# Strassen's seven products for the keys and values of the second attention

## The chip, the cores and the metric

The kernel runs on one core of one Trainium2 chip. The metric is the device time of one execution in microseconds. The engines are TensorE (PE), VectorE (DVE), ScalarE (ACT) and GpSimd (POOL); SP issues most of the transfers. All arithmetic that this change touches is in 32-bit floats.

## The reference

The model is four layers, each a gated attention to a context and a gated feed-forward part, on x of 2 batches x 256 rows x 256 columns. The context has 2 batches x 512 rows x 256 columns. Two layers use the context in a form that matters here:

```python
    # layer 0: the context itself is key and value; layer 1: 16 heads of 128 columns
    def _L1_xattn_ref(inputs_q, inputs_kv, Wq, Wk, Wv, Wo):
        q = (inputs_q @ Wq).reshape(b, sq, H, HD) * (1.0 / np.sqrt(HD))
        k = (inputs_kv @ Wk).reshape(b, skv, H, HD)
        v = (inputs_kv @ Wv).reshape(b, skv, H, HD)
        scores = jnp.einsum('bqhd,bkhd->bhqk', q, k)
        attn = jax.nn.softmax(scores, axis=-1)
        ctx = jnp.einsum('bhqk,bkhd->bqhd', attn, v).reshape(b, sq, H * HD)
        return ctx @ Wo
    x = x + jnp.tanh(g_xattn[1]) * _L1_xattn_ref(_layernorm(x, axis=-1), ctx_2048, ...)
```

So the keys of one head are a product of the context (1024 rows in all, 256 columns) with 256 x 128 weights, and the values likewise. The 256 columns that are summed over are two halves of 128, the height of PE's array.

## The kernel before

The layers run one after the other. The text is Python that lists instructions; the framework then lays out an order for each engine's queue when the program is built, by when it reckons each instruction to be ready, with the place in the text deciding between instructions that are ready together. On the chip each queue runs in that fixed order, with waits on semaphores. A tile of a pool takes one of the pool's buffers at its first writing and gives it back after its last reading. Helpers named `inline` and `behind` pin some orders by hand, in the first attention above all; the second attention has no pins.

PSUM, which PE writes and from which VectorE and ScalarE read, is split during the second attention into `ps_mm` (4 buffers, line 530), `ps_tr` (2 buffers, line 531, for transposes) and `ps_acc` (2 buffers). In SBUF the pools `q2` (15 buffers of 2 KB per partition) and `q4` (11 of 4 KB) hold working tiles, and `slab` has 12 slots for weights.

The context lies in SBUF twice: `ctx_nat` (rows on partitions) is read by the scores of the first attention (line 438) and again at the end by the fourth attention (line 1248), which begins its reading at 527 us; `ctxT` (columns on partitions, two halves `k`) is read by all key and value products and by others.

The first attention (`l0_scores`, `l0_values`, `l0_join`, `l0_exchange`, `l0_finish`) ends on PE at about 56 us. The values of head group 0 (`l1_values_of(0)`, line 555) follow, then the first feed-forward part (`ternary_ffn`), whose signs GpSimd prepares in `ternary_below` (line 348) while the first attention runs.

The second attention has 16 heads in 4 groups `g` of 4 heads `hl`. A group's weights (queries, keys, values, output) are one load of 2 MB into two slots of the slab (`load_group`). For a head, in the order of the text (lines 673 to 691):

- queries: 2 products of 512 columns into one buffer of `ps_mm`, copied by ScalarE (line 681);
- for each batch `b`: `l1_scores`, 4 products of 256 columns into two buffers of `ps_mm`, exponentials by ScalarE (line 643), and their sums over rows by VectorE (lines 646, 647);
- `l1_attend`, one call late through `later`: 4 products of 256 columns with the values and one with ones, the reciprocal and a multiplication on VectorE (lines 655, 656), and two running sums on GpSimd (lines 657, 658), which later tell whether a general form of the kernel must run instead;
- `l1_keys_of(h + 2)`: the keys for the head after the next, for each batch 2 products of 512 columns, summed in PSUM and copied by ScalarE (line 551);
- in the group's second head, `l1_values_of(g + 1)`: 8 times 2 products of 512 columns, copied by ScalarE into slab slots 8 to 11 (line 542);
- after the group, `l1_out` (16 products of 256 columns, added to x on VectorE).

The first group's values and the first two heads' keys are made ahead of the loop. After the loop come the loads of the expert weights of layer 2 into slots 4 to 11 (line 695).

Of the kernel before, what the change touches and what calls it, by code (L numbers as in the profile page):

```python
# [17 lines left out]
F32 = mybir.dt.float32  # L18
# [7 lines left out]
P = 128  # L26
# [3 lines left out]
B = 2  # L30
M = 512
# [18 lines left out]
def flamingo(ctx: ExitStack, tc: tile.TileContext, a: dict, out: bass.AP):  # L50
    nc = tc.nc
# [6 lines left out]
    q4 = pool("q4", Q4)  # L58
    q2 = pool("q2", Q2)
# [32 lines left out]
    slab = const.tile([P, SLOTS, WCOLS], F32, name="slab")  # L92
# [17 lines left out]
    l1_w = [load_group(0), load_group(1)]  # L110
# [149 lines left out]
    def mm(shape=None):  # L260
        return ps_mm.tile(shape or [P, 512], F32, tag="mm", name="mm")
# [221 lines left out]
    for s in range(18):  # L483
# [3 lines left out]
        if 1 <= s <= 16:  # L487
            m, i, half = (s - 1) // 4, (s - 1) // 2 % 2, (s - 1) % 2
# [45 lines left out]
    HD = 128  # L534

    def l1_values_of(g):
        v = slab[:, 8 + 2 * (g % 2) : 10 + 2 * (g % 2), :].rearrange("p s (m c) -> p (s m) c", m=4)
        for mt in range(8):
            p = mm()
            chain(p, [(ctxT[:, mt // 4, k, mt % 4 * P : (mt % 4 + 1) * P], l1_w[g][2][:, k, :])  # L540
                      for k in range(2)])
            nc.scalar.copy(v[:, mt, :], p)  # L542
        return v

    def l1_keys_of(h):
        kT = q4.tile([P, B * M], F32, tag="q4", name="kT")
        for b in range(B):
            p = mm()
            chain(p, [(l1_w[h // 4][1][:, k, (h % 4) * HD : (h % 4 + 1) * HD], ctxT[:, b, k, :])
                      for k in range(2)])  # L550
            nc.scalar.copy(kT[:, b * M : (b + 1) * M], p)  # L551
        return kT


    v_next = l1_values_of(0)

    def transposed(pr, dst, view=None):
        tr = ps_tr.tile([P, 4, P], F32, tag="tr", name="tr")
        for c in range(4):
            inline(nc.tensor.transpose(tr[:, c, :], pr[:, c * P : (c + 1) * P] if view is None else view(pr, c), ident), pe_line)  # L560
        evict(dst, tr)
# [12 lines left out]
    def ternary_ffn():  # L574


        xs = [q4.tile([P, B, 2, 256], F32R, tag="q4", name="xs") for _ in range(2)]

        def split(n, tr):
            top = q1.tile([P, 2, P], F32, tag="q1", name="topx")  # L580
            nc.vector.tensor_scalar(top.bitcast(I32), tr.bitcast(I32), -4096, None, ALU.bitwise_and)
            nc.scalar.copy(tokens(xs[0], n), top)
            nc.vector.tensor_sub(tokens(xs[1], n), tr, top)

        norm_tiles(split, xn0)
# [12 lines left out]
        ps = {}  # L598
        for c, _, ts in by_batch(FCH):
            if c not in ps:  # L600
                ps[c] = mm(), mm()
            for w, p in zip((0, 2), ps[c]):
                chain(p[:, ts], [(signs[w + k][:, c * P : (c + 1) * P], batch(h, k, ts)) for k in range(2) for h in xs])
            if ts.stop == T:
                s = q2.tile([P, T], F32, tag="q2", name="silu")
                nc.scalar.activation(s, ps[c][0], AF.Silu, scale=scales[0])
                nc.vector.tensor_mul(s, s, ps[c][1])
                h = q4.tile([P, 2, T], F32R, tag="q4", name="hT")
                halves(h[:, 0, :], h[:, 1, :], s)
                later(lambda c=c, h=h: l0_down(c, h), 1)  # L610
        flush()
        for dh in range(2):
            p = outs[dh]
            o = q2.tile([P, T], F32, tag="q2", name="o0")
            nc.scalar.copy(o, p)
            tr = ps_tr.tile([P, NT, P], F32, tag="tr", name="tr")
            for n in range(NT):
                nc.tensor.transpose(tr[:, n, :], o[:, n * P : (n + 1) * P], ident)
            cols = x[:, :, dh * P : (dh + 1) * P]
            nc.vector.scalar_tensor_tensor(cols, tr, s2, cols, ALU.mult, ALU.add)  # L620


    ternary_ffn()
    l1_w += [load_group(2), load_group(3)]
    keys = deque(l1_keys_of(h) for h in range(2))
# [8 lines left out]
    def l1_scores(b, qT, kT):  # L634
        cols = slice(b * 256, (b + 1) * 256)
        es = []
        for half in range(2):
            s = mm([P, 2, D])
            for k in range(2):
                c = b * M + (2 * half + k) * P  # L640
                chain(s[:, k, :], [(kT[:, c : c + P], qT[:, cols])])
            e = q2.tile([P, 2, D], F32, tag="q2", name="e1")
            nc.scalar.activation(e, s, AF.Exp)  # L643
            es.append(e)
        t = q2.tile([P, 2, D], F32, tag="q2", name="t1")
        nc.vector.tensor_add(t, es[0], es[1])  # L646
        nc.vector.tensor_add(t[:, 0, :], t[:, 0, :], t[:, 1, :])  # L647
        return es, t

    def l1_attend(b, hl, v, es, t, oT):  # L650
        acc = ps_acc.tile([P, 2, D], F32, tag="acc", name="acc")
        chain(acc[:, 0, :], [(v[:, b * 4 + c, hl * HD : (hl + 1) * HD], es[c // 2][:, c % 2, :]) for c in range(4)])
        chain(acc[:, 1, :], [(ones, t[:, 0, :])])
        r = q1.tile([P, D], F32, tag="q1", name="r1")
        nc.vector.reciprocal(r, acc[:, 1, :])  # L655
        nc.vector.tensor_mul(oT[:, b * 256 : (b + 1) * 256], acc[:, 0, :], r)  # L656
        nc.gpsimd.tensor_add(all_t, all_t, t[:, 0, :])  # L657
        nc.gpsimd.tensor_add(all_r, all_r, r)  # L658

    def l1_out(g, oTs):  # L660
        wo = l1_w[g][3]
        for n in range(NT):
            acc = ps_acc.tile([P, D], F32, tag="acc", name="acc")
            chain(acc, [(oTs[hl][:, n * P : (n + 1) * P], wo[:, hl, :]) for hl in range(4)])
            add_to_x(n, acc, gx(1))

        if g == 0:
            ffn1.extend([load(0, "l1_gate"), load(1, "l1_up")])
        if g == 1:
            ffn1.extend([load(2, "l1_down"), load(3, "l2_attn")])  # L670

    ffn1 = []
    for g in range(4):
        v, oTs = v_next, []
        for hl in range(4):
            h = 4 * g + hl
            kT = keys.popleft()
            qT = q2.tile([P, T], F32, tag="q2", name="qT")
            p = mm()
            chain(p, [(l1_w[g][0][:, k, hl * HD : (hl + 1) * HD], batch(xT, k)) for k in range(2)])  # L680
            nc.scalar.activation(qT, p, AF.Copy, scale=HD ** -0.5)  # L681
            oT = q2.tile([P, T], F32, tag="q2", name="oT")
            oTs.append(oT)
            for b in range(B):
                es, t = l1_scores(b, qT, kT)
                later(lambda b=b, hl=hl, v=v, es=es, t=t, oT=oT: l1_attend(b, hl, v, es, t, oT), 1)
            if h < 14:
                keys.append(l1_keys_of(h + 2))
            if hl == 1 and g < 3:
                v_next = l1_values_of(g + 1)  # L690
        later(lambda g=g, oTs=oTs: l1_out(g, oTs), 2)
    flush()
    gu2 = slab[:, 4:12, :].rearrange("p e (w k i) -> p e w k i", w=2, k=2)
    for e in range(E):
        nc.sync.dma_start(slab[:, 4 + e, :], a["l2_gu_all"][e])
# [329 lines left out]
    t, u = rtile(), place  # L1025
# [1162 lines left out]
```

## Time and profile before

| | us |
|---|---|
| runs before: median of 3 (lowest to highest) | 612.91 (611.39 to 617.0) |
| the profiled execution's own time | 606.47 |
| its span on the core | 604.7 |
| PE busy | 577.8 |
| DVE busy | 279.0 |
| ACT busy | 194.9 |
| POOL busy | 139.9 |
| mean granted PE clock | 0.988 |

The profile is of one execution; its span is 1.8 us shorter than its time. "Busy" is the sum of the stretches in which an engine works; PE's weight loads run beside its products and are listed apart. In the lists, a product of the text with 32-bit floats stands as two matrix instructions. A group of instructions is named by line, engine, operation and tiles (out<-in), with count, busy time and the mean duration of one, and then the idle time ahead of it with what ended that. Line 265 is the helper `chain`, through which most products go.

### The profile page before, as it was taken

The page shows a single profiled execution, that of the slowest core. Times are in us where ns is not written, and L with a number is a line of the kernel's source. Part 1 is how long each engine was busy: PE and PEld are TensorE (multiplying, and loading weights), DVE is VectorE, ACT ScalarE, POOL GpSimd, SP SyncE. Part 2 cuts the span into 40 slices and gives each one's busy share as a digit, 9 for nine tenths or more (in the row PEclk, how much of TensorE's full clock was granted, in tenths as well). Part 3 has the DMA queues.
Part 4 walks back from the last instruction along what each step waited for, and adds up shares of the span by engine and source line. Part 5 has one row for each costly group of instructions (what it writes and reads, how often), then busy time and mean ns, then how long its engine had stood idle before and what let it go on. Part 6 is the DMA issues. An engine that isn't in the chain of part 4 may idle for free.

```text
span 604.7 us, 8168 instructions
## 1 busy us (share of the span) xinstructions
PE 577.8 (96%) x3142; PEld 380.1 (63%) x3142; DVE 279.0 (46%) x575; ACT 194.9 (32%) x369; POOL 139.9 (23%) x238
## 2 busy tenths in 40 slices
PE   8989998999999999999999998999999999899995
PEld 5544674656677466864678677648666445785454
DVE  6967343342534244350445557223566524554323
ACT  6855543433223233123331331220432311332220
POOL 3883152110211112020111213201011000243150
PEclk9979999999999999999999999999999999899998
DMA  8903300000201001010044014603120599804013
GB/s 302 379 2 124 156 0 1 0 1 1 69 2 69 1 0 69 10 60 1 1 140 139 0 70 148 218 15 131 63 65 6 221 419 412 212 22 135 17 41 119
DMA packets 14980, 58.06 MB, mean 96 GB/s; under 512 B 2621, under 2 KB 5892, under 8 KB 11302
## 3 DMA queue, kind: packets, MB, share of 16 engines
q1 hardware_dynamic: 12886, 52.65, 24.0%
q0 software_dynamic: 1472, 4.28, 2.2%
q8 instruction: 27, 0.44, 0.3%
q10 hardware_dynamic: 576, 0.53, 0.3%
q14 instruction: 19, 0.16, 0.1%
HBM read 52.65 MB, written 5.25 MB: 96 GB/s over the span
## 4 chain that ended last, share of the span: by engine, by line
PE 81%; DVE 7%; DMA 4%; POOL 4%; ACT 1%; issue 1%; SPq 0%; POOLq 0%; DVEq 0%
PE mm L265 46%; PE acc L265 18%; PE mm L1106 3%; PE mm L1434 2%; POOL tern L348 2%; DMA slab<-in_l_gu_all 2%; DMA slab<-in_l_gate 2%; PE s L438 2%; PE acc L450 1%; DVE x L268 1%; PE outT L595 1%; PE acc L1127 1%; PE acc L1456 1%; POOL rstd L220 1%; DVE r L655 1%
## 5 line engine op out<-in xcount | busy, mean ns | idle before, releaser
L646 DVE TENSOR_TENSOR t<-e,e 128x512 f32<-128x512 f32 x32 | 26.4, 826 | 138.0 <-ACT e L643 138.0
L265 PE MATMUL mm<-xT,slab 128*128 128x512 f32 (+1 forms) x236 | 85.2, 507 | 0.5 <-ACT xT L249 0.5
L265 PE MATMUL mm<-slab,ctxT 128*128 128x512 f32 x160 | 70.4, 593 | 0.0
L657 POOL TENSOR_TENSOR all_t<-all_t,t 128x256 f32<-128x256 f32 x32 | 23.2, 725 | 189.6 <-DVE t L647 189.6
L265 PEld LDWEIGHTS mm<-xT,slab 128*128 128x128 f32 x236 | 44.1, 190 | 34.9 <-issue 32.0
L265 PE MATMUL mm<-qT,kT 128*128 128x256 f32 x256 | 62.3, 385 | 0.7 <-ACT qT L681 0.7
L265 PE MATMUL acc<-e,slab 128*128 128x256 f32 x256 | 62.9, 379 | 0.0
L643 ACT ACTIVATE e<-mm 128x512 f32<-128x512 f32 x64 | 38.2, 597 | 71.7 <-PE mm L265 71.7
L265 PE MATMUL mm<-ctxT,slab 128*128 128x512 f32 x128 | 57.7, 592 | 0.0
L655 DVE RECIPROCAL r<-acc 128x256 f32<-128x256 f32 x32 | 56.0, 1751 | 1.9 <-PE acc L265 1.6
L265 PEld LDWEIGHTS acc<-e,slab 128*128 128x128 f32 x256 | 48.6, 190 | 13.0 <-issue 7.2
L265 PEld LDWEIGHTS mm<-qT,kT 128*128 128x128 f32 x256 | 47.3, 190 | 10.9 <-ACT qT L681 5.1
L265 PEld LDWEIGHTS mm<-slab,ctxT 128*128 128x128 f32 x160 | 30.2, 190 | 35.6 <-issue 35.3
L551 ACT COPY kT<-mm 128x512 f32<-128x512 f32 x32 | 18.8, 586 | 66.3 <-PE mm L265 65.5
L265 PEld LDWEIGHTS mm<-ctxT,slab 128*128 128x128 f32 x128 | 24.2, 190 | 23.4 <-issue 22.2
L442 ACT ACTIVATE e<-s 128x512 f32<-128x512 f32 x64 | 32.9, 605 | 11.6 <-PE s L438 7.4
L542 ACT COPY slab<-mm 128x512 f32<-128x512 f32 x32 | 18.8, 586 | 38.5 <-PE mm L265 35.4
L219 POOL TENSOR_TENSOR rstd<-mv,eps_ln 128x1 f32<-128x1 f32 x30 | 6.1, 205 | 106.9 <-DVE mv L218 106.9
L658 POOL TENSOR_TENSOR all_r<-all_r,r 128x256 f32<-128x256 f32 x32 | 23.3, 727 | 32.2 <-DVE r L655 32.2
L265 PE MATMUL acc<-slab,oT 128*128 128x256 f32 x128 | 29.1, 381 | 0.7 <-DVE oT L656 0.6
L265 PEld LDWEIGHTS acc<-slab,oT 128*128 128x128 f32 x128 | 24.1, 190 | 4.7 <-DVE oT L656 1.5
L438 PE MATMUL s<-slab,ctx_nat 32*128 32x256 f32 x256 | 23.8, 426 | 2.8 <-ACT e L442 2.0
(306 smaller groups left out, 791.3 us busy)
## 6 DMA issues: line engine op xcount, KB each, us to landing
slab<-in_l_gu_all SPq DMA_DIRECT2D x16, 1024.0 KB, 5.1
slab<-in_l_all SPq DMA_DIRECT2D x4, 2048.0 KB, 21.9
slab<-in_l_dn_all SPq DMA_DIRECT2D x4, 1024.0 KB, 6.0
slab<-in_l_dn_all SPq DMA_DIRECT2D x8, 512.0 KB, 10.0
slab<-in_l_gu SPq DMA_DIRECT2D x4, 704.0 KB, 11.9
slab<-in_l_up SPq DMA_DIRECT2D x2, 1024.0 KB, 6.4
slab<-in_l_gate SPq DMA_DIRECT2D x2, 1024.0 KB, 7.5
slab<-in_l_down SPq DMA_DIRECT2D x2, 1024.0 KB, 5.0
```

The source lines that it names most:

```text
L265: inline(nc.tensor.matmul(dst, lhsT=lhsT, rhs=rhs, start=(i == 0), stop=(i == len(pairs) - 1)), pe_line)
L348: inline(nc.gpsimd.tensor_scalar(t, wi, sc[:, 2:3], None, ALU.is_lt), pool_line)
L438: in_turn(nc.tensor.matmul(ps[j][:, k, :], lhsT=ctx_nat[rows, b, hf, c * P : (c + 1) * P], rhs=qm[rows, n, i, :], start=True, stop=True))
L442: exps.append(nc.scalar.activation(es[j], ps[j], AF.Exp))
L542: nc.scalar.copy(v[:, mt, :], p)
L551: nc.scalar.copy(kT[:, b * M : (b + 1) * M], p)
L643: nc.scalar.activation(e, s, AF.Exp)
L646: nc.vector.tensor_add(t, es[0], es[1])
L655: nc.vector.reciprocal(r, acc[:, 1, :])
L657: nc.gpsimd.tensor_add(all_t, all_t, t[:, 0, :])
L658: nc.gpsimd.tensor_add(all_r, all_r, r)
L1106: inline(nc.tensor.matmul(ps[j * BLK : (j + 1) * BLK, :], lhsT=xsT[k][:, (4 * q + j) * BLK : (4 * q + j + 1) * BLK], rhs=gu2[:, home(q, j) ...
```

## The change

Keys and values of the second attention come from seven products of blocks for eight. A pair of heads (for keys) or a pair of 256-column halves of a group (for values) gives the two column blocks, the two halves of 128 context columns give the blocks that are summed over, and the two batches give the row blocks. The order is the form of Strassen's algorithm with four sums on each side. 

- `context_sums` makes the four sums of context blocks once, on GpSimd, and writes them over `ctx_nat`, which the first attention has finished with by then; it stands in the text ahead of `ternary_ffn`. After the loop `ctx_nat` is loaded again for the fourth attention, ahead of the expert loads.
- `weight_sums` makes the four sums of weight blocks on GpSimd, for each pair of heads (128 x 128 each, in a `q2` tile) and each group (128 x 256 each, in a `q4` tile).
- `seven` issues the products M1 to M7, each into a PSUM buffer of its own, four of them from `ps_tr`, and puts the results together with one copy on ScalarE and seven additions on VectorE, each with one operand in PSUM. It is a generator in three pieces: M1, M2; M6, M5; M7, M3, M4.
- In the loop an even head runs one half of the next group's values and an odd head the keys of the next two heads, one piece behind each batch's scores and the third behind the head's last `later`. Heads 12, 14 and 15 run none.
- The first group's values and the keys of heads 0 and 1 are made as before.

```diff
@@ -554,6 +554,96 @@
     v_next = l1_values_of(0)
 
+    ctx_sums = ctx_nat.rearrange("p b h c -> p (b h) c")
+
+    def context_sums():
+        t = [ctx_sums[:, i, :] for i in range(4)]
+        (b0, b0_), (b1, b1_) = ([ctxT[:, b, k, :] for k in range(2)] for b in range(B))
+        nc.gpsimd.tensor_sub(t[0], b1, b0)
+        nc.gpsimd.tensor_sub(t[1], b1_, t[0])
+        nc.gpsimd.tensor_sub(t[2], b1_, b1)
+        nc.gpsimd.tensor_sub(t[3], b0_, t[1])
+
+    def weight_sums(pool, tag, u, v):
+
+        cols = u.shape[2]
+        t = pool.tile([P, 4, cols], F32, tag=tag, name="wsum")
+        nc.gpsimd.tensor_add(t[:, 0, :], v[:, 0, :], v[:, 1, :])
+        nc.gpsimd.tensor_sub(t[:, 1, :], t[:, 0, :], u[:, 0, :])
+        nc.gpsimd.tensor_sub(t[:, 2, :], u[:, 0, :], v[:, 0, :])
+        nc.gpsimd.tensor_sub(t[:, 3, :], u[:, 1, :], t[:, 1, :])
+        return t
+
+    def seven(u, v_, s, ctx_of, product, view, out):
+
+        b0, b0_, b1, b1_, t1, t2, t3, t4 = ctx_of
+        (c11, c12), (c21, c22) = out
+
+        def one(w, t, tr=False):
+            p = view(ps_tr.tile([P, 512], F32, tag="tr", name="mm_t") if tr else mm())
+            product(p, w, t)
+            return p
+
+        m1 = one(u[0], b0, True)
+        m2 = one(u[1], b0_)
+        nc.scalar.copy(c12, m1)
+        nc.vector.tensor_add(c11, c12, m2)
+        yield
+        m6 = one(s[1], t2, True)
+        m5 = one(s[0], t1)
+        nc.vector.tensor_add(c21, c12, m6)
+        nc.vector.tensor_add(c12, c21, m5)
+        yield
+        m7 = one(s[2], t3, True)
+        m3 = one(s[3], b1_)
+        nc.vector.tensor_add(c21, c21, m7)
+        nc.vector.tensor_add(c22, c21, m5)
+        nc.vector.tensor_add(c12, c12, m3)
+        m4 = one(v_, t4, True)
+        nc.vector.tensor_add(c21, c21, m4)
+        yield
...
+    def seven_keys(p):
+
+        w = l1_w[p // 2][1]
+        u, v = (w[:, :, (2 * p + i) % 4 * HD : ((2 * p + i) % 4 + 1) * HD] for i in range(2))
+        s = weight_sums(q2, "q2", u, v)
+        kT = [q4.tile([P, B * M], F32, tag="q4", name="kT") for _ in range(2)]
+        keys.extend(kT)
+
+        def product(dst, w, t):
+            nc.tensor.matmul(dst, lhsT=w, rhs=t, start=True, stop=True)
...
+    def seven_values(g):
...
+        s = weight_sums(q4, "q4", u, z)
+
+        def product(dst, w, t):
+            for j in range(2):
+                nc.tensor.matmul(dst[:, j, :], lhsT=t[:, j * P : (j + 1) * P], rhs=w, start=True, stop=True)
...
+        return v, [two(m) for m in range(2)]
...
@@ -620,6 +710,7 @@
+    context_sums()
     ternary_ffn()
@@ -681,15 +772,22 @@
             oTs.append(oT)
+            if hl == 0 and g < 3:
+                v_next, sets = seven_values(g + 1)
+            todo = sets[hl // 2] if hl % 2 == 0 else seven_keys(h // 2 + 1) if h < 14 else None
             for b in range(B):
                 es, t = l1_scores(b, qT, kT)
+                if todo:
+                    next(todo)
                 later(lambda b=b, hl=hl, v=v, es=es, t=t, oT=oT: l1_attend(b, hl, v, es, t, oT), 1)
-            if h < 14:
-                keys.append(l1_keys_of(h + 2))
-            if hl == 1 and g < 3:
-                v_next = l1_values_of(g + 1)
+            if todo:
+                next(todo)
         later(lambda g=g, oTs=oTs: l1_out(g, oTs), 2)
+        if g == 2:
+            sets = [None, None]
     flush()
+    for b in range(B):
+        load_context(nc.sync, ctx_nat, b)
```

More of the change, by code (lines that the diff above doesn't have):

```diff
@@ new lines, in context_of @@
+    def context_of(ts):
+        return [ctxT[:, b, k, ts] for b in range(B) for k in range(2)] + [ctx_sums[:, i, ts] for i in range(4)]
+    def seven_keys(p):
[6 more added lines that the diff above has]
+            nc.tensor.matmul(dst, lhsT=w, rhs=t, start=True, stop=True)
+        return seven([u[:, k, :] for k in range(2)], v[:, 1, :], [s[:, i, :] for i in range(4)],
+                     context_of(slice(0, M)), product, lambda t: t,
+                     [[t[:, b * M : (b + 1) * M] for b in range(B)] for t in kT])
@@ new lines, in seven_values, with two @@
+    def seven_values(g):
+        v = slab[:, 8 + 2 * (g % 2) : 10 + 2 * (g % 2), :].rearrange("p s (m c) -> p (s m) c", m=4)
+        w = l1_w[g][2]
+        u, z = (w[:, :, i * 256 : (i + 1) * 256] for i in range(2))
+        s = weight_sums(q4, "q4", u, z)
+        def product(dst, w, t):
+            for j in range(2):
+                nc.tensor.matmul(dst[:, j, :], lhsT=t[:, j * P : (j + 1) * P], rhs=w, start=True, stop=True)
+        def two(m):
+            return seven([u[:, k, :] for k in range(2)], z[:, 1, :], [s[:, i, :] for i in range(4)],
+                         context_of(slice(2 * m * P, 2 * (m + 1) * P)), product, lambda t: t.rearrange("p (j c) -> p j c", j=2),
+                         [[v[:, b * 4 + 2 * m : b * 4 + 2 * m + 2, i * 256 : (i + 1) * 256] for b in range(B)] for i in range(2)])
+        return v, [two(m) for m in range(2)]
```

## The prediction

> **What bounds the kernel now.** I read the page's busy shares first, then the table of stretches, then the chain that ended last. On the page TensorE (PE) is the fullest engine; in the stretch of the second attention, 104 to 371 us, it is full.
>
> ```profile
> PE 577.8 (96%) x3142; PEld 380.1 (63%) x3142; DVE 279.0 (46%) x575; ACT 194.9 (32%) x369; POOL 139.9 (23%) x238
> ```
>
> ```profile
> 104.00:371.00 267.00, 265.60 (x953) 179.17 (x951) 113.05 (x147) 79.54 (x133) 46.93 (x65) 1.00 0.12 42
> ```
>
> The columns are PE, PE weight load, VectorE (DVE), ScalarE (ACT), GpSimd (POOL), granted clock, DMA share. PE lacks 1.4 us of 267 at full clock, VectorE works 42% of the time, GpSimd 18%. A busy PE need not be one at its peak, so I take prices from the chain of waits, where the time from one group's start to the next is what the engine really takes:
>
> ```profile
> 112.21 5.15 PE mm L265 x12
> 117.36 0.86 PE acc L265 x4
> 118.23 1.82 PE mm L265 x8
> 120.04 1.29 PE acc L265 x6
> 121.34 1.73 PE mm L265 x8
> 123.07 2.16 PE acc L265 x10
> 125.22 18.88 PE mm L265 x44
> ```
>
> Each product of the text appears twice in the trace. The first line is the keys of a coming head (8) and a head's queries (4), all 512 columns wide: 5.15/12 = 0.429 us each. The line of 44 is 8 keys, 32 values, 4 queries: again 0.429; the next such line starts at 197.97, a group's period of 72.75 us. The ten of 2.16 us (a head's sum over values, 256 wide, each with its own weights) give 0.216. So cost goes by columns, 0.86 us per product of the text at 512 and 0.43 at 256, and the pieces join without a gap: whatever PE no longer does here shortens the kernel, unless a new wait takes its place.
>
> **What it removes from PE.** Keys: a pair of heads took 8 products of 512, now 7: 0.86 us less, for 7 pairs (heads 2 to 15): 6.0 us. Values: a group took 32 entries of 0.429 = 13.73 us; now 2 x 7 x 2 products of 256 = 56 entries x 0.2155 = 12.07: 1.66 less, for 3 groups: 5.0 us. Together **-11.0 us**. The half-width price is taken from the row of the same shape (weights changed at every product).
>
> **What it adds to VectorE.** Thirteen calls of `seven` (7 key pairs, 6 halves of values), seven adds of 128x512 each with one operand in PSUM. Nearest row, one SBUF and one PSUM operand:
>
> ```profile
> L607 DVE TENSOR_TENSOR silu<-silu,mm 128x512 f32<-128x512 f32 x8 | 5.5, 685 | 10.1 <-PE mm L265 8.3 <-ACT silu L606 1.8
> L655 DVE RECIPROCAL r<-acc 128x256 f32<-128x256 f32 x32 | 56.0, 1751 | 1.9 <-PE acc L265 1.6 <-issue 0.3
> L551 ACT COPY kT<-mm 128x512 f32<-128x512 f32 x32 | 18.8, 586 | 66.3 <-PE mm L265 65.5 <-POOL hT L362 0.8
> L362 POOL TENSOR_TENSOR hT<-silu,top 128x512 fp32r<-128x512 f32 x8 | 10.3, 1292 | 20.6 <-DVE top L360 20.6
> L657 POOL TENSOR_TENSOR all_t<-all_t,t 128x256 f32<-128x256 f32 x32 | 23.2, 725 | 189.6 <-DVE t L647 189.6
> ```
>
> 7 x 0.685 = 4.8 us a call, 62 us in all; ScalarE loses three of every four copies of 0.586, 23 us. A head now costs VectorE 2 x (0.83 + 0.43 + 1.75 + 0.42) = 6.9 (its two batches: both adds of exponentials, reciprocal, multiply) plus 4.8 = 11.7 us, against PE's 1.72 queries + 3.45 scores + 4.32 sums + 6.0 seven products = 15.5 us. 75% full: cover, if the order holds. Walked from the head's start at 0 with these prices: queries to 1.7, M1 to 2.6, scores of batch 0 to 4.3, M2 to 5.2, the previous head's sum to 7.3, scores of batch 1 to 9.0, M6 and M5 to 10.8, sum of batch 0 to 12.9, M7, M3, M4 to 15.5. VectorE gets M6 at 10.1, but takes the exponentials of batch 1 first and adds M6 by 12.1, M5 by 12.8; then the reciprocal and multiply of batch 0 (ready at 13.1) to 15.3, then M7's sum to 16.0, M5's second to 16.7, M3's to 17.4, M4's to 18.1. Who waits: M4 needs M6's bank at 14.6 (spare 2.5 us); the next head's M1 needs M7's bank at 17.2 (spare **1.2**); its second score half needs M5's at 18.9 (2.2); its batch 1 needs the last key sum at 22.8. So the added adds cost **0** on the path, with 1.2 us as the smallest cover in each call.
>
> Could the adds be dearer while GpSimd sums beside them? An add of two SBUF tensors is:
>
> ```profile
> 120.77 0.69 DVE L646 TENSOR_TENSOR t<-e,e 128x512 f32<-128x512 f32 x1 [6.30 <-ACT e L643]
> 123.74 0.73 POOL L658 TENSOR_TENSOR all_r<-all_r,r 128x256 f32<-128x256 f32 x1 [0.94 <-DVE r L655]
> 123.97 1.04 DVE L646 TENSOR_TENSOR t<-e,e 128x512 f32<-128x512 f32 x1
> ```
>
> 0.69 alone, 1.04 beside a GpSimd sum. The PSUM adds lie between 0.685 and 1.04; I take 0.685, since L607 ran at 0.676 to 0.689 in a stretch where GpSimd's L362 was at work. At 1.04 the cover of 1.2 shrinks to about 0.4, and still nothing shows. [...]
>
> **What it adds to GpSimd.** Per key pair four differences of 128x128, at most half of L657's 0.725: 0.4 each, 1.6 us. Per group four of 128x256: 2.9 us. A head's own load is 4 x 0.725 = 2.9, so at most 5.8 of 15.5. The first sum that PE needs is at 9.0 us into the head: hidden. If late, M6 would wait, and M5 behind it.
>
> The four context sums of 128x512 (L362's 1.29 each) are another matter. They overwrite the copy of the context that the first attention reads, tile by tile, so the first is free to run early, on a queue that is then the chain:
>
> ```profile
> 27.18 6.56 POOL L348 TENSOR_SCALAR tern<-slab,tq_sc 128x1024 f32<-128x1024 f32 x2
> 33.71 0.72 POOL L524 TENSOR_TENSOR all_t<-all_t,mixed 128x256 f32<-128x256 f32 x1
> ```
>
> ScalarE stood 3.96 us for that L524. One sum placed ahead of it costs **+1.3**; the second could at worst do the same (+2.6); none, 0. The others come free when GpSimd sits idle (5.75 us before 50.8 in its timeline) or under the values of group 0 (to 67.5). I take 1.3.
>
> **Small edits.** Head 0: PE idled 0.7 us for the first queries' copy; M1 of the values can stand there: **-0.7** (0 to -1.2, with the 0.46 before it). Heads 12 to 15 have less to fill waits with, but heads 14 and 15 ran without keys before at no visible gap: 0. The two reloads of the context (0.5 MB each, landing in 10.5 us in the beginning by the DMA list) go into SP's queue ahead of expert loads not used before 469 us in the chain and are themselves read at 527: 0; without that cover some 10 us.
>
> **Sum.** -11.0 + 1.3 - 0.7 = **-10.4 us**. The profiled execution took 606.5 us (span 604.7, 1.8 around it): 596.1. The median of the runs shown is 612.9, 6.4 above it; the same difference gives **602.5**.
>
> **Rivals.**
> 1. *VectorE becomes the bound (slower).* Place: M4 and the next M1 stand until VectorE has returned their bank. If its fixed order puts one more reciprocal and multiply (2.17) and an add (0.69) ahead of M7's sum, that is 2.86 - 1.2 = 1.7 us late, 13 times: +21.6, so 624.1. It cancels the gain from 0.8 us per call and loses 1% from 1.3. For it: the reciprocal at 1.75 us is four times a multiply, and an order reckoned with a cheaper one would be wrong. Against it: the same order, made the same way, left 1.4 us of gaps before, and the walk has room.
> 2. *Half the gain is lost in small waits.* 0.4 us per call (5.2) and both context sums on the chain (2.6): -11.0 - 0.7 + 7.8 = -3.9: 609.0. For it: two banks for four of the seven products; against it: PE can put a ready sum in front, as it does at 117.36.
> 3. *The change doesn't do what it says for values.* If a 256-wide product cost 13.73/56 = 0.245, only the keys gain: -6.0 + 1.3 - 0.7 = -5.4: 607.5. Against it: ten in 2.16 us, repeated in every head.
>
> **Chances.** Forecast 0.72, first rival 0.10, second 0.12, third 0.06. A measurement of this kernel can tell about 1% (6.1 us) from no change. The third lies near that limit and is halved: faster 0.75, same 0.15, slower 0.10. The range 598 to 612 takes the forecast with its bounds (-12.2 to about -8.4) and the scatter of the runs around it, and rivals two and three; the first is left out.
>
> **What would show it.** Right: PE as full as before in the second attention, the stretch 11 to 12 us shorter, group period 72.8 down to about 69.4, VectorE near 70% there; PSUM adds at 0.69. Wrong: gaps on PE released by VectorE ahead of M4 or M1 (rival 1), a first attention longer by more than 1.3 us, half-width products at other than 0.216.

## The result, and the profile after

| | before | after |
|---|---|---|
| median of the runs, us (lowest to highest) | 613.69 (611.39 to 617.0) | 597.01 (596.26 to 599.61) |
| the profiled execution's own time | 606.47 | 596.37 |
| its span | 604.7 | 594.6 |

The ratio of the runs is 0.975 with a 95% interval of 0.972 to 0.979: faster by 2.5%. A second comparison (experiment 5) gave 597.95 against 608.81, a ratio of 0.983 (0.978 to 0.988). The kernel after keeps its place between 597 and 598; the kernel before moves between medians of 609 and 614 from one comparison to the next (experiments 1 to 4, 5 to 8 and 9 to 12 each ran on a chip of their own). The ratios leave out a few disturbed runs, and so do the medians of the comparison of experiments 9 to 12, where one run took 753.55 us. The two profiled executions differ by 10.1 us.

The engines of the page after:

```profile
PE 567.5 (95%) x3200; PEld 390.9 (66%) x3200; DVE 331.8 (56%) x666; ACT 172.1 (29%) x330; POOL 165.6 (28%) x282
```

PE works 10.3 us less in 58 more instructions, VectorE 53 us more, GpSimd 26 more, ScalarE 23 less. The stretch of the second attention in the table of stretches (columns: PE, PE weight load, DVE, ACT, POOL, granted clock, DMA share, GB/s):

```profile
104.00:360.00 256.00, 255.59 (x1014) 190.49 (x1013) 163.59 (x239) 56.81 (x95) 67.54 (x104) 1.00 0.14 47
```

PE stands still for 0.4 us of 256, where it stood 1.4 of 267 before. VectorE is at 64%. The chain of waits after shows the group period and the beginning of the stretch:

```profile
104.60 1.98 PE mm L265 x4
106.59 0.86 PE mm_t L638 x4
107.45 1.82 PE mm L265 x8
...
174.77 5.18 PE acc L265 x24
...
244.22 5.18 PE acc L265 x24
...
312.38 5.18 PE acc L265 x24
```

The first three lines are head 0's queries, then M1 of the values, which fills the time in which the queries are copied, then the scores: no gap. The lines of 24 are the ends of the groups: 69.45 us from the first to the second (72.75 before) and 68.16 to the third (the last group makes no further values). One head in the same chain:

```profile
133.49 1.72 PE mm L265 x4
...
136.07 1.82 PE mm L265 x8
...
138.75 2.16 PE acc L265 x10
140.91 1.73 PE mm L265 x8
142.64 0.86 PE mm_t L638 x4
```

The queries are 0.43 each, the sums over the values 0.216 each, as before, and the four 256-wide entries of a values product (`mm_t`, L638) take 0.86, so 0.215 each. The prices of the new work, by groups (line, engine, operation, tiles, count | busy, mean ns of one | idle time ahead):

```profile
L606 DVE TENSOR_TENSOR kT<-kT,mm 128x512 f32<-128x512 f32 x7 | 4.8, 681 | 0.0
L595 DVE TENSOR_TENSOR slab<-slab,mm 128x512 f32<-128x512 f32 x6 | 4.1, 681 | 6.7 <-PE mm L638 6.7
L577 POOL TENSOR_TENSOR wsum<-wsum,slab 128x128 f32<-128x128 f32 x7 | 3.2, 454 | 0.0
L737 DVE TENSOR_TENSOR t<-e,e 128x512 f32<-128x512 f32 x32 | 23.8, 744 | 51.3 <-ACT e L734 50.5
```

An addition with an operand in PSUM takes 0.63 to 0.68 us, and a weight sum of 128x128 0.45.

**Where the time went.** Three marks divide the runs: the first sum of the first attention on GpSimd (L524), the start of the copy of head 0's queries on ScalarE, and the first silu of the feed-forward part behind the second attention. Read from the timelines of all kernels, in us:

```
                    queries copied   first silu   between
before                  105.7          385.6       279.9
before, again           109.6          389.5       279.9
after                   106.6          374.2       267.6
after, again            107.6          375.2       267.6
keys alone              107.7          380.6       272.9
values alone            109.8          383.3       273.5
```

The stretch repeats to 0.1 us, and in it the change is worth 12.3 us. What lies around it moves by several us from run to run of the same kernel: 105.7 and 109.6 at the head, and 219.1 and 226.2 us from the first silu to the end, both of the kernel before. So the difference of 10.1 us of the two profiled executions is 12.3 of gain less 0.9 us ahead of the stretch and some 1.3 us in all behind it, of a size that two runs of one kernel also show.

### The profile page after: what moved, and what is told of

The parts are those of the page before. It is cut to its first block, busy times and chain, and to the rows that moved or that the text cites. A ratio compares the mean times of both kernels' runs of the same rounds, so it can differ in the third digit from the quotient of the medians.

```text
span 594.6 us, 8405 instructions
## 1 busy us (share of the span) xinstructions
PE 567.5 (95%) x3200; PEld 390.9 (66%) x3200; DVE 331.8 (56%) x666; ACT 172.1 (29%) x330; POOL 165.6 (28%) x282
## 4 chain that ended last, share of the span: by engine, by line
PE 82%; DVE 7%; POOL 5%; DMA 3%; issue 2%; ACT 1%; SPq 0%; POOLq 0%; DVEq 0%
PE mm L265 32%; PE acc L265 19%; PE mm_t L623 4%; PE mm L1204 4%; PE mm_t L638 3%; PE mm L623 3%; PE mm L638 3%; PE mm L1532 2%; POOL tern L348 2%; PE acc L1225 2%; DMA slab<-in_l_gate 2%; PE acc L450 2%; DVE x L268 1%; PE s L438 1%; PE outT L685 1%
## 5 line engine op out<-in xcount | busy, mean ns | idle before, releaser
L734 ACT ACTIVATE e<-mm 128x512 f32<-128x512 f32 x64 | 38.1, 597 | 83.0 <-PE mm L265 83.0
L265 PE MATMUL acc<-e,slab 128*128 128x256 f32 x256 | 61.0, 379 | 0.0
L737 DVE TENSOR_TENSOR t<-e,e 128x512 f32<-128x512 f32 x32 | 23.8, 744 | 51.3 <-ACT e L734 50.5
L772 ACT ACTIVATE qT<-mm 128x512 f32<-128x512 f32 x16 | 9.6, 597 | 106.7 <-PE mm L265 106.7
L265 PE MATMUL mm<-slab,ctxT 128*128 128x512 f32 x64 | 28.7, 594 | 0.0
L268 DVE SCALAR_TENSOR_TENSOR x<-acc,tg,x 128x256 f32<-128x256 f32 x28 | 13.4, 477 | 25.7 <-PE acc L265 25.6
L1204 PE MATMUL mm<-slab,xsT 128*32 128x512 f32 x192 | 22.6, 595 | 0.2 <-ACT xsT L1159 0.2
L438 PEld LDWEIGHTS s<-slab,ctx_nat 32*128 32x128 f32 x256 | 15.0, 197 | 10.1 <-issue 5.6
L265 PEld LDWEIGHTS mm<-slab,ctxT 128*128 128x128 f32 x64 | 12.0, 190 | 12.6 <-issue 12.4
```

The lines of the kernel that those rows point to most:

```text
L265: inline(nc.tensor.matmul(dst, lhsT=lhsT, rhs=rhs, start=(i == 0), stop=(i == len(pairs) - 1)), pe_line)
L268: return inline(nc.vector.scalar_tensor_tensor(x[:, n, cols], acc, scalar, x[:, n, cols], ALU.mult, ALU.add))
L438: in_turn(nc.tensor.matmul(ps[j][:, k, :], lhsT=ctx_nat[rows, b, hf, c * P : (c + 1) * P], rhs=qm[rows, n, i, :], start=True, stop=True))
L1204: inline(nc.tensor.matmul(ps[j * BLK : (j + 1) * BLK, :], lhsT=xsT[k][:, (4 * q + j) * BLK : (4 * q + j + 1) * BLK], rhs=gu2[:, home(q, j) ...
```

## The experiments

### 1 to 4: the kernel before, the two halves alone, the first context sum later

The kernel before ran again without an edit. Keys alone:

```diff
-            if hl == 0 and g < 3:
-                v_next, sets = seven_values(g + 1)
-            todo = sets[hl // 2] if hl % 2 == 0 else seven_keys(h // 2 + 1) if h < 14 else None
+            todo = seven_keys(h // 2 + 1) if hl % 2 and h < 14 else None
...
+            if hl == 1 and g < 3:
+                v_next = l1_values_of(g + 1)
```

Values alone:

```diff
-            todo = sets[hl // 2] if hl % 2 == 0 else seven_keys(h // 2 + 1) if h < 14 else None
+            todo = sets[hl // 2] if hl % 2 == 0 else None
...
+            if h < 14:
+                keys.append(l1_keys_of(h + 2))
```

The first context sum behind all sums of the first attention, by a pin:

```diff
-        nc.gpsimd.tensor_sub(t[0], b1, b0)
+        behind(nc.gpsimd.tensor_sub(t[0], b1, b0), l0_pool, "behind the sums of the first attention")
```

> The kernel before, unchanged, to see where its own time varies. The changed kernel's profiled execution is 10.1 us below the profiled one of before (596.37 against 606.47), but its median is 15 to 17 us below (597.0 against 612.9 or 613.7). Theory A: the second attention saves 12 us in every execution, and the rest is scatter of before outside it (the waits for expert loads between 470 and 530 us and the gather and scatter at the end); then another profile of before shows the second attention from its first queries to the first product of the feed-forward part behind it at 277.5 us again (103.66 to 381.21), and a span somewhere between 604 and 615 whose difference lies behind 430 us. Theory B: the second attention itself is slower in most executions of before; then that stretch reads 280 to 283 us. Time: ratio 1.00 against before under both.

> Seven products for the keys alone; values as before, all sixteen products of a group in its second head. Theory A (cost by columns, VectorE hidden): the stretch from the first queries to the feed-forward part shortens by 7 x 0.86 = 6.0 us, first queries about 1 us later for the context sums on GpSimd; profiled time about 601, ratio 0.985 to 0.992. Rival (the gain comes mostly from the finer mixing of the pieces, or from values): less than 3 us, ratio above 0.995.

> Seven products for the values alone; keys as before, two products summed in PSUM for each batch. Theory A: 3 x 1.66 = 5.0 us off the second attention, and some 0.7 us more because M1 can stand in the first head's wait for its queries; context sums cost 1 us ahead of it; profiled time about 601.5, ratio 0.985 to 0.993. Rival (256-wide products cost more than half): 1 us or less off, ratio above 0.997.

> The changed kernel with the four context sums queued on GpSimd behind the last running sum of the first attention (at about 62 us) and not in front of the signs at 18.7 us. Theory A (the first of them cost 1.1 us on the chain through GpSimd): the first queries of the second attention start at 103.5 to 103.8 us, not 104.6; the second attention is as long as in the changed kernel; profiled time 595.3, 1.1 less. Rival (the later start has another cause, the weights' transfer that the chain begins with): first queries at 104.6 again, time unchanged; and if the sums come too late for the first halves of the feed-forward part, up to 2 us slower.

Measured against 611.92 in one comparison: before again 612.33 (ratio 1.001, 0.998 to 1.005), keys alone 604.06 (0.987, 0.982 to 0.992), values alone 608.47 (0.992, 0.989 to 0.996), the sum later 599.07 (0.978, 0.973 to 0.983). In the marked stretch the keys give 7.0 us and the values 6.4, where the products were reckoned at 6.0 and 5.0. The stretches, queries to silu, of before, after, keys alone and values alone:

```profile
105.70:385.60 279.90, 276.25 (x1008) 189.20 (x1009) 118.70 (x162) 82.19 (x138) 52.80 (x80) 1.00 0.14 49
```

```profile
106.60:374.20 267.60, 264.95 (x1064) 199.35 (x1064) 168.88 (x253) 59.11 (x99) 71.56 (x116) 1.00 0.16 55
```

```profile
107.70:380.60 272.90, 269.62 (x991) 186.16 (x992) 145.36 (x211) 69.27 (x116) 64.78 (x108) 1.00 0.16 54
```

```profile
109.80:383.30 273.50, 270.85 (x1077) 201.90 (x1076) 144.35 (x204) 71.43 (x120) 58.36 (x88) 1.00 0.16 54
```

PE's busy time falls from 276.25 by 6.6 (keys) and 5.4 (values), to 264.95 with both (11.3), and its idle time from 3.65 to 3.3, 2.65 and 2.65. So some 11 us of the 12.3 are products and about 1 is idle time. The halves add up to 1.1 us more than the whole, 0.35 of it in idle time and 0.7 in busy time. Since the ends of products are modelled, I don't split these tenths further, and why they don't add up is not shown.

The fourth run prices the context sum. GpSimd's timeline, after and then with the sum later:

```profile
18.74 1.40 POOL L567 TENSOR_TENSOR ctx_nat<-ctxT 128x512 f32<-128x512 f32 x1
...
28.74 6.12 POOL L348 TENSOR_SCALAR tern<-slab,tq_sc 128x1024 f32<-128x1024 f32 x2
34.82 0.72 POOL L524 TENSOR_TENSOR all_t<-all_t,mixed 128x256 f32<-128x256 f32 x1
```

```profile
19.09 5.80 POOL L348 TENSOR_SCALAR tern<-slab,tq_sc 128x1024 f32<-128x1024 f32 x2
...
27.82 6.56 POOL L348 TENSOR_SCALAR tern<-slab,tq_sc 128x1024 f32<-128x1024 f32 x2
34.35 0.72 POOL L524 TENSOR_TENSOR all_t<-all_t,mixed 128x256 f32<-128x256 f32 x1
```

The sum takes 1.40 us and stands in the chain ahead of `tern`. From the first part of that chain (VectorE's `tq_part`, L327) to L524 it is 20.76 us before, 21.54 after, 20.75 with the sum later: the sum costs 0.8 us there, not 1.3, mostly because the second pair of `tern` behind it took 6.12 us and not 6.56. Yet the expected gain of the whole didn't come: 599.07 (after itself did not run in this comparison), a span of 597.2 against 594.6, and head 0's queries copied at 108.8, where after has 106.6 and 107.6. The 0.8 us is smaller than what the granted clock takes from run to run, which is told at the end: in this execution 3.4 us at half clock fell on the query products, which took 2.98 us in place of 1.98.

### 5 to 7: does VectorE become the bound?

By the walk of the prediction the smallest cover was 1.2 us a call, and a return of banks later than that by 0.8 us was to cancel the gain. The additions were therefore made longer, by needless ones ahead of M7's sum (the last addition writes the same tile anew, so the results stay): none, three and seven a call.

```diff
         m3 = one(s[3], b1_)
+        for _ in range(7):
+            nc.vector.tensor_add(c22, c21, m5)
         nc.vector.tensor_add(c21, c21, m7)
```

> The changed kernel again, unchanged, against more runs of before. The profiles of before (two of them) and of the changed kernel put the second attention, from the first query copy to the first activation of the feed-forward part behind it, at 279.9, 279.9 and 267.6 us: 12.3 less; the context sums cost 0.8 on GpSimd's chain ahead of it. Theory A: 11.5 us of 612 in all, ratio 0.981, and the 0.975 of the first four runs was helped by scatter outside the attention. Theory B: the change also makes something outside the attention faster by some 4 us in most executions; then the ratio stays at 0.975 or below and the profile shows a stretch behind the attention that is shorter than in both profiles of before.

> The changed kernel with three more additions of 128x512 on VectorE in each of the thirteen calls, one operand in PSUM, ahead of M7's sum (into the block that M5's second addition then overwrites): 2.06 us a call, 27 us of VectorE in all. Theory A (VectorE's work is covered, with a least cover of 1.2 us by the walk; in the changed kernel's trace M7's sum ended about 1.8 us ahead of the next M1): the bank comes back up to 0.3 us late, so 0 to 4 us slower than the changed kernel, and 7 us or more still left of the gain: ratio to before 0.981 to 0.988. Rival (VectorE already sets the pace, so that every addition shows): 27 us slower, ratio 1.02 or more.

> Seven more such additions a call, 4.8 us, so that VectorE needs 16.5 us for a head of 15.5 us of products. Theory A (cover up to a point, then the bound): at least 13 x 1.0 = 13 us slower than the changed kernel, at most 13 x (4.8 - 1.8) = 39; time between 610 and 638, VectorE over 90% busy in the second attention, gaps on TensorE that VectorE's additions end. Rival (the order gives way, other work fills in): under 5 us slower.

Measured against 608.81: 597.95 (0.983, 0.978 to 0.988), 597.05 (0.978, 0.974 to 0.983) and 597.86 (0.982, 0.977 to 0.988). The additions cost nothing, even seven of them: 4.5 us of VectorE a call, nearly four times the cover. The same stretch with seven:

```profile
106.60:374.10 267.50, 264.86 (x1064) 199.49 (x1063) 226.97 (x344) 59.00 (x99) 71.73 (x116) 1.00 0.16 55
```

VectorE went from 168.9 to 227.0 us, 85% of the stretch, and the stretch stayed. My theory was a walk of one fixed order with the products of a late bank standing in it. But the order isn't fixed ahead of the sizes: it is laid out anew when the program is built, with the longer additions in it. In the timeline of after, M1 of the next values stands at 135.05, ahead of the scores:

```profile
135.05 1.03 PE L638 MATMUL mm_t<-slab,ctxT 128*128 128x256 f32 x4
```

With seven more additions, other products stand there and M1 comes 4 us later, without a gap of PE:

```profile
135.06 1.03 PE L265 MATMUL acc<-e,slab 128*128 128x256 f32 x4
...
135.39 2.12 DVE L605 TENSOR_TENSOR kT<-kT,mm 128x512 f32<-128x512 f32 x3
...
137.55 0.69 DVE L606 TENSOR_TENSOR kT<-kT,mm_t 128x512 f32<-128x512 f32 x1
...
139.04 1.03 PE L640 MATMUL mm_t<-slab,ctxT 128*128 128x256 f32 x4
```

(`acc<-e,slab` is a ready sum over values; L605's three are needless additions, L606 is M7's, which frees the bank.) So a late bank moves M1 behind work that is ready, and there is such work as long as VectorE keeps up as a whole.

### 8: the seven products for the first group too

```diff
+    v_next, sets = seven_values(0)
+    for todo in sets:
+        for _ in todo:
+            pass
     ternary_ffn()
...
-    keys = deque(l1_keys_of(h) for h in range(2))
+    for _ in seven_keys(0):
+        pass
```

The first context sum moves behind the first attention's sums of the first tile, and `l1_values_of(0)` goes.

> The changed kernel with the seven products also for the first group's values and the first two heads' keys, and the first context sum queued behind the first attention's first running sum, not ahead of the signs. Theory A (cost by columns where products fill TensorE): 1.66 + 0.86 us less products, 0.8 less on GpSimd's chain: up to 3 us faster than the changed kernel, ratio about 0.977. Rival (here the products were cover for the normalization that VectorE does between the first attention and the first feed-forward part, and the 14 plus 7 additions now stand in the same queue): a gap ahead of the feed-forward part's transposes and no gain or up to 4 us slower than the changed kernel, ratio 0.981 to 0.988.

Measured: 603.4 against 608.81 (0.991, 0.988 to 0.994), where after stood at 597.95: about 5 us lost, with 2.5 us of products saved. The second attention is as in after (267.7 us); the queries of head 0 are copied at 113.2 in place of 106.6 to 107.6. Experiments 11 and 12 take it apart.

### 9 and 10: where VectorE does become the bound

The same needless additions, fourteen and ten a call.

> What it leaves as it is: all results. Fourteen needless sums are put ahead of M7's in every call of the seven products. Seven needless ones added 91 instructions and took VectorE's work between the first copied query and the second feed-forward part from 168.9 to 227.0 us of 267.5, 0.64 us each, and cost no time; 182 of them make 285 us, more than the stretch. Theory (only the sum of the work counts, the order of the products gives way until VectorE's work is longer than TensorE's): the stretch grows to VectorE's own length, 285 to 290 us, so 18 to 22 us slower than the changed kernel, about 615 to 620 us, VectorE busy for over 97% of it. Rival (it counts by the head: the calls stand in 13 of 16 heads, there VectorE has some 10.6 + 8.9 = 19.5 us against TensorE's 16.7, and the three heads without a call can't take any of it over): 13 x 2.8 = 36 us slower, about 634 us, and VectorE at 95% or less. A third way, that it costs nothing still, can't be by the sum.

> Ten needless sums in every call. 130 of them at 0.64 us make VectorE's work 252 us of 267.6 (94%). Theory (only the sum counts): no time, 0 to 2 us slower than the changed kernel. Rival (by the head): 10.6 + 6.4 = 17.0 us on VectorE against 16.7 on TensorE, and with waits that come to both, 4 to 8 us slower.

Measured against 612.79: 663.7 (1.083, 1.073 to 1.092) and 606.0 (0.989, 0.984 to 0.994). Their stretches are 333.1 and 273.8 us, against 267.6: 65.5 and 6.2 us longer.

```profile
108.40:382.20 273.80, 268.23 (x1065) 197.84 (x1063) 244.10 (x383) 59.02 (x99) 70.50 (x116) 1.00 0.16 54
```

```profile
106.00:439.10 333.10, 289.58 (x1064) 207.30 (x1063) 279.47 (x435) 59.13 (x100) 70.30 (x116) 0.93 0.13 45
```

The theory that only the sum of VectorE's work counts is wrong: with ten its sum is 89% of the stretch and time is lost already. Worked out by the head (168.9/16 = 10.6 us of a head's work in after, a mean over all heads, and the needless additions spread over the 13 heads with a call), VectorE has 15.0 us with seven, 16.4 with ten and 19.1 with fourteen, against PE's 16.7 (267.6/16): 90%, 98%, 114%. The bound lies between the first two. The rival by the head was right on ten (4 to 8 us), but its 36 us on fourteen are little more than half of what came. Of the 65.5 us PE stands still for 40.9 more than in after (43.5 against 2.65); the rest, 24.6, is PE working longer on the same products. The clock column shows part of why: 0.93 on the mean. One place in PE's timeline with fourteen:

```profile
212.87 1.02 PE L625 MATMUL mm<-ctxT,wsum 128*128 128x512 f32 x2
...
221.24 2.08 PE L625 MATMUL mm_t<-ctxT,slab 128*128 128x512 f32 x2 [5.19 <-DVE slab L606]
223.11 2.96 PE L625 MATMUL mm_t<-ctx_nat,wsum 128*128 128x512 f32 x4
225.91 1.02 PE L625 MATMUL mm_t<-ctx_nat,slab 128*128 128x512 f32 x2
```

M1 waits 5.19 us for M7's bank (L606), just as rival 1 of the prediction described it; then the same product takes 2.08 us in place of 1.02, and for some 4 us all do. Read in slices of one us, the stretch has seven standstills of 2.4 us and more, and each comes with a piece of 6.8 us at a clock of 0.50: 48 us in all, so by an estimate at most 24 us of lost products, against the 24.6 (in the piece above PE stands still for the first 2.8 us). These standstills are paid a second time in slow products.

### 11 and 12: the first keys alone, the first values alone

The two halves of experiment 8's diff by themselves; the values bring the moved context sum with them.

> The changed kernel with the first two heads' keys by the seven products as well, nothing else. With all of the first group by the seven products, the time from the first product of the ternary layer to the first copied query went from 36.2 to 42.2 us: 1.6 us more until the layer's last silu (at a granted clock of 0.83 in ten of these us), 4.4 more behind it, where VectorE had the sums of the keys' blocks between the pieces of the normalization and TensorE stood still for 3.4 of 13 us. Theory (the sums stand ahead of the normalization's own steps on VectorE, where TensorE has nothing else to do): the 4.4 us are the keys' and return here, 40 to 41 us from the first ternary product to the first copied query, 3.5 to 4.5 us slower than the changed kernel less the 0.9 us of the two products saved. Rival (the 4.4 us come from the values' sums, which push the whole layer back): no more than 1 us slower or even 0.9 faster, 35 to 37 us.

> The changed kernel with the first group's values by the seven products as well and the keys of the first two heads by the eight, the first sum of the context behind the first attention's sums of the first tile. Theory (as for the keys: twelve sums at 0.67 us, 8 us of VectorE, ahead of the ternary layer's xn and xs, with VectorE without a gap from 57.6 to 69.4 us and TensorE standing still for 1.7 us in front of the transposes): what the products save, 1.7 us, is lost there; 0 to 1 us slower than the changed kernel; 35.5 to 37 us from the first attention's first sum to the first ternary product, 36 to 36.5 from there to the first copied query. Rival (the values' sums bring the whole loss of 5 to 6 us): 40 us or more in one of the two. Rival on the other side (the values' sums are hidden behind the weights' transfer of the layer): 1 to 1.7 us faster.

Medians against the same 612.79: 602.48 (0.981, 0.973 to 0.988) and 602.27 (0.982, 0.974 to 0.989). The kernel after didn't run in this comparison, so I go by the stretches, in us (L360 takes the high bits of a silu of the ternary layer, the last one near its end):

```
                  (a) L524 to first   (b) from there to   (c) from there to   clock,
                  ternary product     the last L360       the queries' copy   36 to 54 us
after                  35.6                21.8                  14.3            0.91
first keys             36.1                21.8                  19.5            0.91
first values           37.7                23.3                  14.4            0.86
both (8)               36.7                23.5                  18.8            0.91
```

The loss is the sum of two, each in its place. The keys cost 5.2 us at the end, where the theory had the loss (41.3 us from the first ternary product to the queries; 40 to 41 expected). But only 2.3 us of it are there when PE's last wait for the normalization (L224) ends. The other 2.9 come behind that, where PE has two more transposes to do and the clock is at 0.50: the query products take 3.35 us in the chain in place of 1.98. In experiment 8 the same two parts are 2.4 and 2.1 us. The values cost 1.5 us in the ternary layer and about 1 ahead of it at an equal clock (experiment 8): more than the 0 to 1 us of the theory. VectorE and PE with the first values, at the change to the ternary layer:

```profile
67.69 0.68 DVE L607 TENSOR_TENSOR slab<-slab,mm 128x512 f32<-128x512 f32 x1
68.29 0.68 DVE L606 TENSOR_TENSOR slab<-slab,mm 128x512 f32<-128x512 f32 x1
68.89 0.42 DVE L672 TENSOR_SCALAR topx<-tr 128x256 int32<-128x256 int32 x1
69.22 0.68 DVE L609 TENSOR_TENSOR slab<-slab,mm_t 128x512 f32<-128x512 f32 x1
```

```profile
70.05 0.74 PE L236 MATMUL tr<-ident,xn 128*128 128x128 f32 x4 [1.68 <-DVE slab L609]
```

The transposes share their two banks with the products that are returned by L609, and `topx`, the next step of the layer, stands in VectorE's queue between the block sums. PE has nothing else to do there and stands 1.68 us. What the theory lacked is what the stretches of one us show a moment later (clock in the third column from the end):

```profile
72.00:73.00 1.00, 1.00 (x7) 1.00 (x7) 0.15 (x1) 0.00 (x0) 0.00 (x0) 0.50 0.06 16
73.00:74.00 1.00, 1.00 (x6) 1.00 (x6) 0.70 (x2) 0.67 (x2) 0.00 (x0) 0.50 0.00 0
```

The clock is halved from 71.8 to 75.2 us, 3.4 us long, which by an estimate costs up to 1.7 us of products: about the 1.5 us lost in the ternary layer. The same seven products that are free inside the second attention cost more than they save ahead of it, because there the normalization is the chain and nothing fills PE's waits. No version that ran is measurably faster than the change as it stands, which leaves the first group alone.

## Why the prediction was right, and where it was off

**Right.** The product term: -11.0 forecast, and PE's busy time in the stretch is 11.3 us less. The half-width price (0.2155 taken, 0.215 measured) rules out rival 3; values alone gave 6.4 us. The additions: 0.685 taken, 0.63 to 0.681 measured, also beside GpSimd's sums, so the upper price of 1.04 wasn't touched (L606 at 149.77 us took 0.68 while `wsum` was summed); the 32 additions `t<-e,e`, with both operands in SBUF, took 0.684 to 1.044, 0.744 on the mean. The walk of a head: M7's sum was to end 16.0 us into the head and the next M1 to start at 17.2; the trace of the second head has 15.5 and 17.3, a cover of 1.8 us. The group period was to be 69.4 and is 69.45. The weight sums (0.4 taken, 0.45 measured) and the reloads of the context show nowhere on the chain.

**Head 0 and the gaps: -0.7 taken.** M1 does fill the wait, and the idle time fell by 1.0 us in all. The stretch gained 12.3 against 11.7 of the sum without the context sum.

**The first context sum: +1.3 taken, 0.8 measured.** What was off is the price: the step was put ahead of a chain at its own full length, but the `tern` pair behind it ran 0.4 us shorter.

**The median: 602.5 forecast, 597.0 measured.** The sum fits the profiled execution (596.1 against 596.37), but so closely by luck: the second attention gave 12.3 us where 11.7 were summed, the context sum took 0.8 where 1.3 were taken, 1.3 us that the sum doesn't have were lost behind the second attention, and a second profiled execution of each kernel took 617.52 (before) and 595.24 (after). The step from there to the median added 6.4 us, by which the kernel before stood above its profiled execution; the kernel after stands only 0.6 above its own. The profiled execution of before was at the low edge of its runs: medians of 609 to 614 were measured for it, 2 to 7 us above 606.5. The range's low end of 598 lay 1 us above the measured median for the same reason. The time of before moves in the parts around the second attention, and part of that is the half clock told of below; why the medians of before stand so far above its first profiled execution, and those of after do not, is open.

**VectorE as the bound (rival 1): the mechanism is real, its point was wrong.** The prediction had the gain cancelled at 0.8 us per call. With 4.5 us more per call nothing was lost, and only with 5.8 us per call, where VectorE has 98% of PE's time per head, 6.2 us were. The step that failed is to price a late bank by the walk of one order: the order is laid out for the longer work, and ready products go in front. VectorE was at 64% of the second attention, below the 70% forecast. **Half lost in small waits (rival 2):** no; PE's idle time fell.

## What to carry to other kernels

Where one engine is full without gaps, count its columns: the group's period came out at 69.45 us where 69.4 were forecast, and the work that replaced them was free on engines with room, up to 90% of the full engine's time per head, not by the cover of one wait in one order. The same replacement loses where the full engine waits on a chain (a normalization, a change of layers): there the added additions stand in that chain, and a standstill of PE can be paid twice (about 5 us lost in experiment 8; in experiment 9, 40.9 us more of standing still and 24.6 of longer products). Price a change against the stretch it is in, between two marks that repeat, since whole runs of this kernel scatter by as much as the change is worth.

## What the runs showed of the hardware

**Half clock, mostly behind a short standstill.** The clock of 0.87 that before shows in the first attention is no constant of this stage. From 36 to 54 us, the stretches of before, before again, after, and the sum later (one line each; after again has a clock of 0.81 there too):

```profile
36.00:54.00 18.00, 18.00 (x206) 9.61 (x203) 12.47 (x18) 12.43 (x25) 11.36 (x10) 0.87 0.01 2
```

```profile
36.00:54.00 18.00, 16.35 (x177) 9.37 (x179) 11.68 (x21) 11.51 (x23) 10.93 (x9) 0.81 0.01 2
```

```profile
36.00:54.00 18.00, 17.78 (x206) 9.40 (x206) 13.76 (x23) 13.64 (x27) 13.77 (x13) 0.91 0.01 2
```

```profile
36.00:54.00 18.00, 18.00 (x196) 9.50 (x195) 11.78 (x20) 13.07 (x26) 11.17 (x10) 0.81 0.01 2
```

Stretches of one us show two values only, 1.00 and 0.50, with the change of state inside a slice between them. PE waits for ScalarE's exponentials, and these for L524, once between 33 and 39 us (1.73 us in before, 1.11 in after). With that wait the clock goes to 0.50, for 3.4 us in after (37.6 to 41.0), and for 6.8 us in before (33.9 to 40.7), before again (38.1 to 45.0), after again (36.0 to 42.8) and with the sum later (36.3 to 43.1). In after:

```profile
36.00:37.00 1.00, 0.78 (x6) 0.58 (x10) 1.00 (x2) 1.00 (x3) 1.00 (x2) 1.00 0.00 0
...
38.00:39.00 1.00, 1.00 (x12) 0.51 (x16) 0.93 (x3) 1.00 (x4) 0.00 (x0) 0.50 0.00 0
39.00:40.00 1.00, 1.00 (x12) 0.23 (x8) 0.01 (x2) 0.58 (x2) 0.84 (x3) 0.50 0.00 0
...
41.00:42.00 1.00, 1.00 (x23) 0.50 (x20) 1.00 (x1) 0.42 (x1) 1.00 (x1) 1.00 0.00 0
```

So, by an estimate from half of 3.4 and of 6.8 us, the same wait costs up to 1.7 us or 3.4 us of products, in two executions of one kernel, and this hides what 0.8 us on GpSimd's chain is worth. In slices of one us every piece of half clock in the profiles of before and after lasts 3.4 or 6.8 us, but for the last of each, which runs into the end of the kernel. By the mean clocks (0.988 over 604.7 us, 0.977 over 615.7) the profile of before has some 14 us of it in all, that of before again some 28; half of the difference is some 7 us, an estimate of what the clock makes at most of the 11.0 us between their spans. The length of a standstill alone doesn't tell whether the clock falls. In the run with the first values PE stood 1.68 and 0.62 us between 68.4 and 71.4, with transposes between, and fell to half clock at 71.8, and in after 1.1 us of waiting between 35 and 36.3 us came ahead of the fall at 37.6. Yet 1.1 us between 69.1 and 70.3 us of the same execution left the clock at 1.00, and so did the standstills of up to 1.5 us in the stretch with fourteen additions. Ahead of the same transposes PE stood 2.25 us in before (until 516.5) and 2.24 in after (until 506.1): the clock went to 0.50 at 518.6 in the first and stayed at 1.00 in the second. And from 454.0 to 457.4 us of after it was at 0.50 without a wait of PE of more than 0.43 us in the ten us ahead of it. What decides it is open.
